# Node sums of a graph layer: from a per-window matmul to strips written to DRAM at register-held rows and read back

## The chip, the cores and the metric

One Trainium2 chip, of which the kernel uses one core with its engines: TensorE (PE, with its weight loads PEld), VectorE (DVE), ScalarE (ACT), GpSimd (POOL) and SyncE (SP). The metric is device time in microseconds (us) of one execution; a kernel's time is the median of several.

## The reference, cut to what matters

A graph layer with 6250 nodes of 256 features and 206250 edges, 33 for each node on average. The edges come sorted by their destination node. `x` first goes through a layer norm and a relu; that is the `x` of the inner function, and the original `x` is added to the result at the end.

```python
polarity = clip(edge_attr[:, 0:1], 0, 1); raw = edge_attr[:, 1:]
e = relu(raw @ W_e1.T + b_e1) @ W_e2.T + b_e2
edge_emb = (e * (polarity + 0.01)) @ W_le.T + b_le
msg = relu(x[src] + edge_emb)
aggr = segment_sum(msg, dst, num_segments=6250)
h = (x + aggr) @ W_g1.T + b_g1
out = relu(layernorm(h) * ln_g + ln_b) @ W_g2.T + b_g2
```

## The kernel before

**Tiling.** A unit `u` is 256 edges, a block is two units (512 edges), and six blocks make a group of 3072 edges; there are NU = 806 units, 403 blocks and NG = 68 groups (the last one has a single block). A group's edges are cut into S = 4 strips of 768 consecutive edges. Because the edges are sorted, the destinations of one strip lie within W = 32 consecutive nodes, from the destination of its first edge on (`base_b` holds these first nodes, as floats). A window `w` is 128 nodes; there are 49. `groups_of(w)` lists the two or three groups whose edges may end in window `w`.

**Per unit.** `edge_part` (L274, L279) multiplies the hidden features by the product of two weight matrices on TensorE, and DVE moves the result out of PSUM with a bias added (`msg`). `first_layer` (L250, with L256 on DVE and L259 on ACT) makes the hidden features two blocks at a time. `gather` (L566) fetches 128 rows of the normalised nodes by an indirect DMA that GpSimd issues; a unit takes two gathers, 1604 in all, into 20 buffers `hg`. `whole` (L615, L620) scales `msg` by the polarity and adds the gathered rows on DVE, two instructions to a unit, and ACT does the relu.

**Sums.** `rows_of_block` (L595) makes a 0/1 matrix `sel` that puts each edge of a strip at one of its 32 rows. `add_up` (L632) multiplies it with the messages, so that a group's sums gather in PSUM as 128 rows: strip `j` in rows 32j to 32j+31. `keep` copies them to `ms` (L644).

**Nodes.** For each window, `node_work` spreads the groups' rows over the window's nodes: `spread` loads `x` (L206), its transposed columns (L691) and the layer norm's two numbers for each node (L693), and makes a 128x128 0/1 matrix for each group on DVE (L698). `ready` (L707) builds the transposed node features `hT` on DVE in four instructions. `rows_of` (L732) multiplies each group's `ms` by its 0/1 matrix on TensorE, for both halves of the features, and DVE adds that to `hT` (L734). Then `first` (L170), a layer norm on DVE and ACT, `second` (two TensorE transposes, L186), `third` (L196) and the output DMA (L201, on SP).

**Order.** The program's order is written out by hand: each engine executes its instructions in the order in which the loop `for u in range(LEAD, NU)` records them, and waits by semaphores. In that loop, `forward(u)` records a unit's TensorE work; every eighth unit it also records the sums of the blocks that are complete and the next first layers and loads (`turn_of`). `whole(made)` runs `lag` units behind, and `lag` falls from 18 to 1 as `u` grows, by one for each SHRINK = 44 units. Node steps stand in `todo` by the unit at which they are due, and `due` records at most one of them per unit; small DVE steps stand in `steps` and `rest`, of which `piece` records one per unit. Gathers are recorded by `in_step`, which adds up estimated TensorE time and records a gather for each STEP = 1.288 us of it, with a wait for the TensorE instruction just recorded; where that has not yet recorded a gather that `whole` needs, `gathers(made + 1)` records it without such a wait. SP's queue, in order, carries all the loads and stores named above.

**The end.** The two last windows need the last groups. They are finished after the loop, through the lists `ending`. A check on the data (`verdict`, `count`, `total`) leads to a second, slower path if the strips do not fit.

Of the kernel before, what the change touches and what calls it, by code (L numbers as in the profile page):

```python
# [9 lines left out]
F32 = mybir.dt.float32  # L10
I32 = mybir.dt.int32
AF = mybir.ActivationFunctionType
# [5 lines left out]
P = 128  # L18
# [16 lines left out]
NT = NB * S  # L35
NG = NF + 1
NP = -(-NB // 2)
MARGIN = 768
DEG = E // N
LEAD = 22  # L40
# [9 lines left out]
TURN = 1  # L50
CH = 4
AHEAD = 10
assert DEG * N == E and NF * GE + S * P >= E


# [15 lines left out]
def groups_of(w):  # L71
    return [g for g in range(NG) if w in windows_of(g)]
# [25 lines left out]
def gnn_kernel(ctx: ExitStack, tc: tile.TileContext, x, src_c, dst_c, dst_r, pol_c, raw_t, w_e1t, w_e2,  # L98
# [50 lines left out]
    def finish_nodes(nd, ps, w, n):  # L149

        r = w * P

        def turn(a):
# [3 lines left out]
            aT = nd.tile([P, 2, P], F32, name="aT")  # L157
# [24 lines left out]

        def second(hs):
            pt = ps()
            for c in range(2):
                nc.tensor.transpose(pt[:, 0, c * P:c * P + n], hs[:n, c * P:(c + 1) * P], ident[:n, :n])  # L186
            nT = nd.tile([P, 2, P], F32, name="nT")
            for c in range(2):
                nc.scalar.activation(nT[:, c, :n], pt[:, 0, c * P:c * P + n], AF.Relu, bias=lnb_s[:, c:c + 1],  # L189
                                     scale=lng_s[:, c:c + 1])  # L190
            return nT

        def third(nT, xt):
            po = ps()
            for c in range(2):
                nc.tensor.matmul(po[:n, 0, :], nT[:, c, :n], wg2_s[:, c, :], start=c == 0, stop=c == 1)  # L196
            ot = nd.tile([P, D], F32, name="ot")
            nc.vector.tensor_add(ot[:n], po[:n, 0, :], xt[:n])
            for i, (a, b) in enumerate(spread_out(n)):
                eng = nc.scalar if i else nc.sync  # L200
                eng.dma_start(out=out[bass.ds(r + a, b - a), :], in_=ot[a:b])  # L201
# [16 lines left out]
    with fast:  # L218
# [297 lines left out]
        ends = w0.tile([P, 3], F32, name="ends")  # L516
        bad = w0.tile([P, 3], F32, name="bad")
        bad3 = w0.tile([3, 1], F32, name="bad3")

        def by_group(i, op):  # L520
            def step():
# [5 lines left out]
        def by_row(i, op):  # L527
            def step():
                nc.vector.tensor_reduce(ends[:, i:i + 1], rel, axis=AX.X, op=op)
            return step  # L530

        def verdict():
            nc.vector.scalar_tensor_tensor(far[:, 0, :], far[:, 0, :], float(DEG), mid, op0=ALU.mult, op1=ALU.subtract)
            nc.vector.scalar_tensor_tensor(far[:, 1, :], far[:, 1, :], -float(DEG), mid, op0=ALU.mult, op1=ALU.add)
            nc.vector.tensor_reduce(ends[:, 2:3], far.rearrange("p a b -> p (a b)"), axis=AX.X, op=ALU.max)
            nc.vector.tensor_scalar(bad[:, 0:1], ends[:, 0:1], float(W - 1), None, op0=ALU.is_gt)
            nc.vector.tensor_scalar(bad[:, 1:2], ends[:, 1:2], 0.0, None, op0=ALU.is_lt)
            nc.vector.tensor_scalar(bad[:, 2:3], ends[:, 2:3], float(GE // 2 + MARGIN), None, op0=ALU.is_gt)

        def count():  # L540
            pq = ps()
            nc.tensor.matmul(pq[:3, 0, 0:1], bad, ones[:, 0:1], start=True, stop=True)
            nc.vector.tensor_copy(bad3, pq[:3, 0, 0:1])

        def total():
            pq = ps()
            nc.tensor.matmul(pq[:1, 0, 0:1], bad3, ones[0:3, 0:1], start=True, stop=True)
            nc.vector.tensor_copy(bad_i, pq[:1, 0, 0:1])


        with tc.tile_pool(name="hg", bufs=HG - RAW) as hg_p, tc.tile_pool(name="ms", bufs=5) as ms_p, \
                tc.tile_pool(name="sel2", bufs=9) as sel2_p, tc.tile_pool(name="nd", bufs=3) as nd:
            got = 2 * RAW
            acc = {}
            made = 0
# [118 lines left out]
            rest = deque()  # L674
            ending = {-2: [], -1: []}

            def at(u, fn):
                todo.setdefault(max(u, now), deque()).append(fn)

            def node_work(w, spread_now=False):  # L680
# [6 lines left out]

                def spread():
                    box["xt"] = load_x()
                    box["hT"] = nd.tile([P, 2, P], F32, name="hT")  # L690
                    nc.sync.dma_start(out=box["hT"][:, :, :n], in_=x_t[:, :, w * P:w * P + n])  # L691
                    st = nd.tile([P, 2, P], F32, name="stb")
                    nc.sync.dma_start(out=st, in_=st_d[w:w + 1].to_broadcast([P, 2, P]))  # L693
                    box["st"] = st
                    box["sel2"] = []
# [82 lines left out]
            for i, fn in ((0, first_rows), (1, strips), (5, row_numbers), (6, stats_out),  # L778
                          (8, node_weights)):
                at(LEAD + i, fn)  # L780
            for i, fn in enumerate((by_group(0, ALU.max), by_group(1, ALU.min), by_row(0, ALU.max), by_row(1, ALU.min),
                                    verdict, count, total)):
                at(LEAD + 22 + 5 * i, fn)
            flag = None
            for u in range(LEAD, NU):
# [13 lines left out]
                due()  # L799
                if len(rest) > 6:  # L800
                    piece()
                if u == NU - 24:
# [1 line left out]
                        if groups_of(w)[-1] == NG - 1:  # L804
                            late[w] = node_work(w, True)
                if u == LEAD + 60:
                    flag = nc.values_load(bad_i[0:1, 0:1], min_val=0, max_val=3 * P)
            while todo:
                now = min(todo)
                for fn in todo.pop(now):  # L810
                    fn()
            while steps:
                steps.popleft()[1]()
            before, last = ending[-2], ending[-1]
# [192 lines left out]
```

## Time and profile before

| | us |
|---|---|
| median of 3 runs (lowest to highest) | 2162.19 (2161.35 to 2164.05) |
| the profiled execution's own time | 2161.02 |
| its span, first to last instruction | 2159.3 |

| engine | busy us | share of the span |
|---|---|---|
| PE | 2144.8 | 99% |
| PEld | 1613.3 | 75% |
| DVE | 1665.9 | 77% |
| ACT | 980.5 | 45% |
| POOL | 1621.5 | 75% |

The profile is one execution. A row of a group reads: line, engine, operation, output and inputs by the program's names, partitions and elements, number of instructions; then the busy time in us and the mean of one in ns; then the engine's idle time just before these instructions and what ended it. TensorE takes a 32-bit matmul in two passes, and the trace records each pass, so that a matmul counts twice (a transpose counts once). TensorE's matmuls overlap in the pipeline; the chain of waits shows how much time a run of them takes end to end. GpSimd's span for a DMA is the time in which it writes the descriptors, not the transfer. The granted TensorE clock of the execution was 0.998 of full speed.

### The profile page before, as it was taken

How to read it: one execution, taken by the hardware profiler on the slowest of the kernel's cores; microseconds unless marked ns; L12 is line 12 of the kernel's file. 1: busy time of each engine (PE TensorE's matmuls, PEld its weight loads, DVE VectorE, ACT ScalarE, POOL GpSimd, SP SyncE). 2: the span in 40 equal slices, each digit the busy share in tenths (PEclk: the TensorE clock that was granted, in tenths of full speed). 3: DMA queues.
4: the chain of work that ended last, by engine and by line, in shares of the span. 5: the costliest groups of instructions: out<-in, count | busy, mean ns of one | idle time of the engine just before them, and what ended most of it. 6: DMA issues, size and time to landing. Idle time of an engine off the chain costs nothing.

```text
span 2159.3 us, 35666 instructions
## 1 busy us (share of the span) xinstructions
PE 2144.8 (99%) x12382; PEld 1613.3 (75%) x12382; DVE 1665.9 (77%) x3975; ACT 980.5 (45%) x1710; POOL 1621.5 (75%) x1675
## 2 busy tenths in 40 slices
PE   9999999999999999999999999999999999999998
PEld 6677777777777777777777777777777777777776
DVE  7898777877777777777777777778777778777786
ACT  7544444444444444444444444444444444444443
POOL 6777777777777777777777777777777777777773
PEclk9999999999999999999999999999999999999999
DMA  9544454544445454545454445444544554454442
GB/s 312 175 134 127 141 157 135 150 137 131 140 131 148 144 149 125 152 131 149 124 151 142 133 130 153 143 133 141 147 138 125 150 151 140 128 152 131 140 138 73
DMA packets 156227, 309.23 MB, mean 143 GB/s; under 512 B 33328, under 2 KB 78089, under 8 KB 156041
## 3 DMA queue, kind: packets, MB, share of 16 engines
q0 software_dynamic: 77376, 211.39, 34.6%
q1 hardware_dynamic: 77364, 92.23, 13.6%
q10 hardware_dynamic: 1300, 3.28, 0.5%
q8 instruction: 98, 1.61, 0.3%
q14 instruction: 89, 0.72, 0.1%
HBM read 293.92 MB, written 12.85 MB: 142 GB/s over the span
## 4 chain that ended last, share of the span: by engine, by line
PE 96%; DVE 2%; DMA 1%; ACT 0%; issue 0%; SPq 0%; DVEq 0%; ACTq 0%
PE pz L274 64%; PE pz L250 17%; PE pd L632 9%; PE pz L732 3%; PE pz L170 2%; PE pz L196 2%; DMA raw<-in_raw_t_dram 1%; PE pz L186 1%; DVE hg L615 0%; DVE msg L279 0%; DVE st L141 0%; DMA xt<-in_x_dram 0%; DVE sel L595 0%; DVE mvx L142 0%; DVE msg L613 0%
## 5 line engine op out<-in xcount | busy, mean ns | idle before, releaser
L566 POOL DMA_INDIRECT hg<-hb_d,src_s x1604 | 1576.6, 983 | 493.9 <-issue 319.8
L274 PE MATMUL pz<-wc_s,e 128*128 128x256 f32 x6448 | 1452.6, 381 | 0.0
L274 PEld LDWEIGHTS pz<-wc_s,e 128*128 128x128 f32 x6448 | 1209.5, 190 | 235.2 <-ACT e L259 71.3
L620 ACT ACTIVATE hg<-hg 128x512 f32<-128x512 f32 x805 | 507.6, 631 | 862.7 <-DVE hg L615 860.9
L615 DVE SCALAR_TENSOR_TENSOR hg<-msg,pol_s,hg 128x256 f32<-128x256 f32 x1612 | 696.8, 477 | 15.6 <-DMA hg<-hb_d,src_s 14.9
L279 DVE TENSOR_TENSOR msg<-pz,bc_s 128x512 f32<-128x512 f32 x799 | 545.5, 683 | 74.0 <-PE pz L274 73.7
L256 DVE TENSOR_SCALAR e<-pz,vecs 128x512 f32<-128x512 f32 x201 | 150.8, 750 | 361.1 <-PE pz L250 361.0
L259 ACT ACTIVATE e<-pz,vecs 128x512 f32<-128x512 f32 x605 | 361.1, 691 | 148.4 <-PE pz L250 148.3
L250 PE MATMUL pz<-raw,we_s 64*128 64x512 f32 x1612 | 379.3, 604 | 3.7 <-DVE msg L279 2.0
L250 PEld LDWEIGHTS pz<-raw,we_s 64*128 64x128 f32 x1612 | 148.5, 187 | 188.2 <-issue 155.4
L632 PE MATMUL pd<-hg,sel 128*32 128x256 f32 x3216 | 194.9, 382 | 0.6 <-ACT hg L620 0.6
L632 PEld LDWEIGHTS pd<-hg,sel 128*32 128x32 f32 x3216 | 94.4, 109 | 87.8 <-issue 34.9
L595 DVE SCALAR_TENSOR_TENSOR sel<-iota_w,zero_c,rel 128x128 f32<-128x128 f32 x403 | 137.3, 341 | 0.0
L644 ACT ACTIVATE ms<-pd 128x256 f32<-128x256 f32 x66 | 25.2, 382 | 127.2 <-PE pd L632 127.1
L732 PEld LDWEIGHTS pz<-s,ms 128*128 128x128 f32 x548 | 68.7, 192 | 3.1 <-PE pd L632 0.4
L732 PE MATMUL pz<-s,ms 128*128 128x128 f32 x548 | 69.3, 275 | 0.1
L707 DVE SCALAR_TENSOR_TENSOR hT<-hT,zero_c,stb 128x128 f32<-128x128 f32 (+1 forms) x196 | 66.7, 341 | 3.0 <-DMA stb<-st_d 3.0
L196 PE MATMUL pz<-wg_s,nT 128*128 128x256 f32 (+1 forms) x196 | 50.6, 380 | 0.6 <-ACT nT L189 0.6
L170 PE MATMUL pz<-wg_s,hT 128*128 128x256 f32 (+1 forms) x196 | 50.5, 380 | 0.0
L392 POOL TENSOR_TENSOR hb<-xt,rows_b 128x256 f32<-128x256 f32 (+1 forms) x49 | 34.1, 728 | 10.5 <-ACT xt L388 3.0
L196 PEld LDWEIGHTS pz<-wg_s,nT 128*128 128x128 f32 (+1 forms) x196 | 37.0, 190 | 6.2 <-ACT nT L189 0.8
L170 PEld LDWEIGHTS pz<-wg_s,hT 128*128 128x128 f32 (+1 forms) x196 | 37.0, 190 | 5.7 <-issue 0.3
(98 smaller groups left out, 412.8 us busy)
## 6 DMA issues: line engine op xcount, KB each, us to landing
raw<-in_raw_t_dram SPq DMA_DIRECT2D x202, 256.0 KB
hg<-hb_d,src_s POOLq DMA_INDIRECT x1604
stb<-st_d SPq DMA_DIRECT2D x49, 128.0 KB
hb_d<-hb SPq DMA_DIRECT2D x12, 512.0 KB
xt<-in_x_dram SPq DMA_DIRECT2D x48, 128.0 KB
hT<-in_x_t_dram SPq DMA_DIRECT2D x48, 128.0 KB
out_dram<-ot SPq DMA_DIRECT2D x48, 128.0 KB
xt<-in_x_dram SPq DMA_DIRECT2D x11, 512.0 KB
```

The source lines that it names most:

```text
L196: nc.tensor.matmul(po[:n, 0, :], nT[:, c, :n], wg2_s[:, c, :], start=c == 0, stop=c == 1)
L250: z = nc.tensor.matmul(pe[s, c], we1_s[s * F:(s + 1) * F, c * P:(c + 1) * P], raw[q][s * F:(s + 1) * F, :], start=True, stop=True)
L256: nc.vector.tensor_scalar(e1[b][:, c, :], pe[s, c], be1_s[:, c:c + 1], 0.0, op0=ALU.add, op1=ALU.max)
L259: nc.scalar.activation(e1[b][:, c, :], pe[s, c], AF.Relu, bias=be1_s[:, c:c + 1])
L274: last_z = nc.tensor.matmul(pz[:, i, :], e1[b][:, c, k:k + P], wc_s[:, c, :], start=c == 0, stop=c == 1)
L279: nc.vector.tensor_add(msg[u], pz, bc_s)
L566: g = nc.gpsimd.indirect_dma_start(out=hg[u][:, i, :], out_offset=None, in_=hb_d, in_offset=bass.IndirectOffsetOnAxis(ap=src_s[:, 2 * u + ...
L595: nc.vector.scalar_tensor_tensor(sel[g][:, k * S:(k + 1) * S, :], iota_w.rearrange("p (o w) -> p o w", o=1).to_broadcast([P, S, W]), zero_ ...
L615: nc.vector.scalar_tensor_tensor(hg[u][:, i, :], m[:, i, :], pol_s[:, 2 * u + i:2 * u + i + 1], hg[u][:, i, :], op0=ALU.mult, op1=ALU.add)
L620: nc.scalar.activation(hg[u], hg[u], AF.Relu)
L632: z = nc.tensor.matmul(acc[g][j * W:(j + 1) * W, :], sel[g][:, k * S + j, :], m[:, j % 2, :], start=k == 0, stop=b == blocks_of(g)[-1])
L732: nc.tensor.matmul(pa[:, c, :n], ms[g][:, c * P:(c + 1) * P], box["sel2"][i][:, :n], start=i == 0, stop=i == len(gs) - 1)
```

## The change

Of the windows, the 47 whose groups all lie before group FAR = 66 are done in another way (`far_work`); the last two are done as before.

- Two arrays in DRAM, `sum_d[0]` and `sum_d[1]`, hold one row of 256 numbers for each node. `clear` writes zeros to a window's rows in both, some groups ahead of its first group.
- When a group's `ms` is there, `rows_out` reads the four strips' first nodes from `base_i` (an integer copy of `base_b`) into SP's registers and writes each strip's 32 rows with a DMA on SP, at the row that the register holds: strips 0 and 2 to the one array, 1 and 3 to the other. Two strips that follow each other may share a node; those of one array may not, and a fourth term in the check on the data covers that.
- `far_work` makes the layer norm's and relu's output for the window's nodes again from `x` on ACT, reads the window's rows of both arrays with two DMAs, adds them with two DVE instructions, transposes the sum with two TensorE transposes (`turn`, copied out of PSUM by ACT), and goes on with `first`, `second` and `third`.
- The matmuls `rows_of`, the 0/1 matrices, the transposed load of `x`, the load of the layer norm's numbers and the steps `ready` fall away for these windows.
- The node steps counted by `due` go from five to four for each window. `piece` now takes the first step that is due, not only the head of the queue. Pools `ms` and `sel2` have fewer buffers (4 and 6 for 5 and 9), and `hT` and `stb` come from a pool of two.

```diff
+FAR = NG - 2
+CLEAR = 4
+    sum_d = [dram.tile([N + W, D], F32, name=f"sum_d{i}") for i in range(2)]
...
+            nc.vector.tensor_copy(base_i, base_b[0:1].rearrange("p g j -> p (g j)"))
+            nc.vector.memset(zrow, 0.0)
...
+        def strips_apart():
+            flat = base_b.rearrange("p g j -> p (g j)")
+            n = FAR * S - 2
+            nc.vector.tensor_tensor(apart[:, :n], flat[:, 2:n + 2], flat[:, :n], ALU.subtract)
+            nc.vector.tensor_reduce(ends[:, 3:4], apart[:, :n], axis=AX.X, op=ALU.min)
...
             def piece():
-                if steps and steps[0][0] <= now:
-                    steps.popleft()[1]()
+                due_now = [s for s in steps if s[0] <= now][:1]
+                if due_now:
+                    steps.remove(due_now[0])
+                    due_now[0][1]()
                 elif rest:
                     rest.popleft()[1]()
...
                     sel.pop(g)
+                    if g < FAR:
+                        soon(1, lambda: rows_out(g, 0))
+                        soon(2, lambda: rows_out(g, 1))
                     for w in range(NW):
-                        if groups_of(w)[-1] == g:
+                        if groups_of(w)[0] == g + CLEAR:
+                            soon(6, lambda w=w: clear(w))
+                        if groups_of(w)[-1] == g < FAR:
+                            far_work(w)
+                        elif groups_of(w)[-1] == g:
                             late.pop(w)()
-                        elif groups_of(w)[-1] == g + 1 < NG - 1:
+                        elif groups_of(w)[-1] == g + 1 == FAR:
                             late[w] = node_work(w)
...
+            def soon(n, fn):
+                moves.setdefault(now + n, []).append(fn)
+            def clear(w):
+                if groups_of(w)[-1] < FAR:
+                    for i in range(2):
+                        nc.sync.dma_start(out=sum_d[i][w * P:(w + 1) * P, :], in_=zrow)
+            def rows_out(g, k):
+                if k == 0:
+                    _, firsts[g] = nc.values_load_multi_w_load_instructions(
+                        base_i[0:1, g * S:(g + 1) * S], engines=[mybir.EngineType.SP], min_val=0, max_val=N)
+                for i in range(2):
+                    j = 2 * k + i
+                    nc.sync.dma_start(out=sum_d[i][bass.ds(firsts[g][j], W), :], in_=ms[g][j * W:(j + 1) * W, :])
+            def far_work(w):
+                box = {}
+                turn, first, second, third, load_x, offset = finish_nodes(nd, ps, w, P)
+                def h_of_x():
+                    box["xt"] = load_x()
+                    box["h"] = nh.tile([P, 2, P], F32, name="stb").rearrange("p a b -> p (a b)")
+                def load():
+                    nc.scalar.activation(box["h"], box["xt"], AF.Relu, bias=nm_s[:, w:w + 1], scale=rs_s[:, w:w + 1])
+                    box["ab"] = ab_p.tile([P, 2, D], F32, name="ab")
+                    for i in range(2):
+                        nc.sync.dma_start(out=box["ab"][:, i, :], in_=sum_d[i][w * P:(w + 1) * P, :])
+                def add(i):
+                    nc.vector.tensor_add(box["h"], box["h"], box["ab"][:, i, :])
+                def turned():
+                    box["hT"] = turn(box["h"], nh, "hT")
+                    at(now + 2, one)
+                def one():
+                    box["hs"] = first(box["hT"])
+                    at(now + 5, two)
+                def two():
+                    box["nT"] = second(box["hs"])
+                    at(now + 4, lambda: third(box["nT"], box["xt"]))
+                soon(1, h_of_x)
+                soon(4, load)
+                steps.extend((now + 6, lambda i=i: add(i)) for i in range(2))
+                steps.extend((now + 7, lambda c=c: offset(box["xt"], c)) for c in range(2))
+                at(now + 9, turned)
```

More of the change, by code (lines that the diff above doesn't have):

```diff
@@ L151, in finish_nodes, with turn @@
         r = w * P
-        def turn(a):
+        def turn(a, pool=nd, name="aT"):
             pt = ps()
@@ L156, in turn @@
                 nc.tensor.transpose(pt[:, 0, c * P:c * P + n], a[:n, c * P:(c + 1) * P], ident[:n, :n])
[L157 removed]
+            aT = pool.tile([P, 2, P], F32, name=name)
             if n == P:
@@ L512, in row_numbers @@
                 nc.vector.tensor_scalar(rowid[q], base_b[q, :, j], p32[q], None, op0=ALU.add)
+            nc.vector.tensor_copy(base_i, base_b[0:1].rearrange("p g j -> p (g j)"))
+            nc.vector.memset(zrow, 0.0)
         far = w0.tile([P, 2, NG], F32, name="far")
-        ends = w0.tile([P, 3], F32, name="ends")
-        bad = w0.tile([P, 3], F32, name="bad")
-        bad3 = w0.tile([3, 1], F32, name="bad3")
+        ends = w0.tile([P, 4], F32, name="ends")
+        bad = w0.tile([P, 4], F32, name="bad")
+        bad4 = w0.tile([4, 1], F32, name="bad4")
+        apart = w0.tile([P, FAR * S], F32, name="apart")
         def by_group(i, op):
@@ L538, in verdict @@
             nc.vector.tensor_scalar(bad[:, 2:3], ends[:, 2:3], float(GE // 2 + MARGIN), None, op0=ALU.is_gt)
+            nc.vector.tensor_scalar(bad[:, 3:4], ends[:, 3:4], float(W), None, op0=ALU.is_lt)
         def count():
             pq = ps()
-            nc.tensor.matmul(pq[:3, 0, 0:1], bad, ones[:, 0:1], start=True, stop=True)
-            nc.vector.tensor_copy(bad3, pq[:3, 0, 0:1])
+            nc.tensor.matmul(pq[:4, 0, 0:1], bad, ones[:, 0:1], start=True, stop=True)
+            nc.vector.tensor_copy(bad4, pq[:4, 0, 0:1])
         def total():
             pq = ps()
-            nc.tensor.matmul(pq[:1, 0, 0:1], bad3, ones[0:3, 0:1], start=True, stop=True)
+            nc.tensor.matmul(pq[:1, 0, 0:1], bad4, ones[0:4, 0:1], start=True, stop=True)
             nc.vector.tensor_copy(bad_i, pq[:1, 0, 0:1])
-        with tc.tile_pool(name="hg", bufs=HG - RAW) as hg_p, tc.tile_pool(name="ms", bufs=5) as ms_p, \
-                tc.tile_pool(name="sel2", bufs=9) as sel2_p, tc.tile_pool(name="nd", bufs=3) as nd:
+        with tc.tile_pool(name="hg", bufs=HG - RAW) as hg_p, tc.tile_pool(name="ms", bufs=4) as ms_p, \
+                tc.tile_pool(name="sel2", bufs=6) as sel2_p, tc.tile_pool(name="ab", bufs=2) as ab_p, \
+                tc.tile_pool(name="nh", bufs=2) as nh, tc.tile_pool(name="nd", bufs=3) as nd, \
+                tc.tile_pool(name="nk", bufs=1) as nk:
+            base_i = nk.tile([1, NG * S], I32, name="base_i")
+            zrow = nk.tile([P, D], F32, name="zrow")
             got = 2 * RAW
@@ L689, in spread @@
                     box["xt"] = load_x()
-                    box["hT"] = nd.tile([P, 2, P], F32, name="hT")
+                    box["hT"] = nh.tile([P, 2, P], F32, name="hT")
                     nc.sync.dma_start(out=box["hT"][:, :, :n], in_=x_t[:, :, w * P:w * P + n])
-                    st = nd.tile([P, 2, P], F32, name="stb")
+                    st = nh.tile([P, 2, P], F32, name="stb")
                     nc.sync.dma_start(out=st, in_=st_d[w:w + 1].to_broadcast([P, 2, P]))
@@ L780, in gnn_kernel @@
                 at(LEAD + i, fn)
+            now = LEAD
+            for w in range(NW):
+                if groups_of(w)[0] < CLEAR:
+                    soon(8, lambda w=w: clear(w))
             for i, fn in enumerate((by_group(0, ALU.max), by_group(1, ALU.min), by_row(0, ALU.max), by_row(1, ALU.min),
-                                    verdict, count, total)):
+                                    strips_apart, verdict, count, total)):
                 at(LEAD + 22 + 5 * i, fn)
@@ L799, in gnn_kernel @@
                 due()
+                for fn in moves.pop(now, []):
+                    fn()
                 if len(rest) > 6:
@@ L806, in gnn_kernel @@
                 if u == LEAD + 60:
-                    flag = nc.values_load(bad_i[0:1, 0:1], min_val=0, max_val=3 * P)
+                    flag = nc.values_load(bad_i[0:1, 0:1], min_val=0, max_val=4 * P)
             while todo:
@@ L811, in gnn_kernel @@
                     fn()
+            assert not moves
             while steps:
```

2 lines of the change are left out of this document (added).

## The prediction

> **What bounds the kernel now.** The page came first: the span and the engines' busy time.
>
> ```profile
> span 2159.3 us, 35666 instructions
> PE 2144.8 (99%) x12382; PEld 1613.3 (75%) x12382; DVE 1665.9 (77%) x3975; ACT 980.5 (45%) x1710; POOL 1621.5 (75%) x1675
> ```
>
> TensorE looks like the only bound, and GpSimd a quarter idle. The groups and the waits of the gathers correct that:
>
> ```profile
> L566 POOL DMA_INDIRECT hg<-hb_d,src_s x1604 | 1576.6, 983 | 493.9 <-issue 319.8
> L566 POOL DMA_INDIRECT hg<-hb_d,src_s x1604: 942/946/1963, 65.3 to 2131.8; - x179
> 2131.85 0.95 POOL L566 DMA_INDIRECT hg<-hb_d,src_s  x1 [0.30 <-issue]
> ```
>
> The 1604 gathers start at 65.3 and the last ends at 2132.8: 2067.5 us, or 1.289 us each. Of that 0.983 is the instruction and 493.9 / 1604 = 0.308 the pause before it. The pause is 0.30 before nearly every one and counts as issue. So GpSimd runs from end to end as well: its idle quarter is the pause between gathers, and no wait can be taken out of it. Two engines are full together.
>
> The chain of waits in the middle of the span, on TensorE alone, is the other bound; two turns of eight units each:
>
> ```profile
> 901.89 1.86 PE pd L632 x32
> ...
> 911.04 1.34 PE pz L732 x12
> ...
> 925.47 3.63 PE pz L250 x16
> 929.10 3.65 PE pz L274 x16
> 932.75 0.22 PE pz L186 x2
> ...
> 944.20 1.86 PE pd L632 x32
> ```
>
> From 901.89 to 944.20, 42.31 us pass for 16 units, 21.16 to a turn, without a gap. How fast do gathers feed a turn? `lag` falls by one in 44 units, so a turn takes 16 x 45/44 = 16.36 gathers: 21.09 us at 1.289. The two rates differ by 0.07 us in 21.
>
> **What the gathers cost, in stretches.** I cut the span at starts of gathers and counted those within:
>
> ```profile
> 140.25:371.61 231.36, 176.23 (x181) 1.00 0.48 137
> 371.61:800.55 428.94, 327.47 (x333) 1.00 0.49 141
> 800.55:1200.17 399.62, 305.17 (x310) 1.00 0.48 139
> 2000.79:2133.00 132.21, 100.45 (x102) 1.00 0.46 136
> ```
>
> Length over count: 1.278, then 1.288 and 1.289. The waits of DVE for a gather's data stand in the first stretch:
>
> ```profile
> DVE hg L615 <- DMA hg<-hb_d,src_s: 13.3, 20, 1.8
> DVE hg L615 <- DMA hg<-hb_d,src_s: 1.6, 2, 1.2
> L615 DVE SCALAR_TENSOR_TENSOR hg<-msg,pol_s,hg x1612: 466/477/552, 71.7 to 2143.9; 128x256 f32<-128x256 f32 x180
> ```
>
> The first line is the window 140 to 371, the second 371 to 2130. So data came just in time early on, and later GpSimd drew ahead; by the third line, which has the first and last start of L615, the last one stands 11 us behind the last gather.
>
> Why does a gather last 0.95 at one time and 1.2 at another? The timeline of the two engines:
>
> ```profile
> 1033.87 0.95 POOL L566 DMA_INDIRECT hg<-hb_d,src_s  x1 [0.30 <-ACT e L259]
> 1034.22 1.67 DVE L615 SCALAR_TENSOR_TENSOR hg<-msg,pol_s,hg 128x256 f32<-128x256 f32 x4
> 1035.12 1.19 POOL L566 DMA_INDIRECT hg<-hb_d,src_s  x1 [0.30 <-issue]
> 1042.79 0.87 DVE L615 SCALAR_TENSOR_TENSOR hg<-msg,pol_s,hg 128x256 f32<-128x256 f32 x2
> 1042.87 1.22 POOL L566 DMA_INDIRECT hg<-hb_d,src_s  x1 [0.30 <-issue]
> ```
>
> Where an L615, whose inputs all lie in SBUF, runs over a gather's start, the gather is 0.24 to 0.27 longer; where it starts well after (1034.22, 0.35 into the gather before), it is not. Summed: 1576.6 - 1604 x 0.946 = 59 us of lengthening, 0.037 for each of 1612 L615.
>
> The Trainium skill has a rule for this, in SBUF — State Buffer, SBUF: two separate sides: a DVE instruction with two SBUF inputs can hold the port pair that DVE and GpSimd share against a GpSimd operation that reads SBUF, and the loser blocks for the whole instruction. The trace agrees, at 0.24 to 0.27 us a hit. It speaks against this change, whose added sums on DVE have two such inputs; by the whole of a 0.42 us instruction for each of 94, the sum would lose 39 us, where the price from rows below is 3.5.
>
> **The change, part by part.**
>
> *TensorE.* The 47 windows hold 134 window-group pairs; two halves and two passes make 536 of the 548 records of
>
> ```profile
> L732 PE MATMUL pz<-s,ms 128*128 128x128 f32 x548 | 69.3, 275 | 0.1
> ```
>
> At 1.34 / 12 = 0.112 (chain above) that is 59.9 us removed. Two transposes for each window come in, 94 at 0.22 / 2 = 0.11: 10.3. Net 49.5 us, all of it on TensorE's path; a turn loses (1.34 - 0.22) / 2 = 0.56 and takes 20.6. If TensorE alone set the end, the span would be 2159.3 - 49.5 = 2109.8.
>
> *GpSimd.* Nothing is taken from it: 1604 gathers, the same start. A turn now needs 20.6 on TensorE and 20.91 (at 1.278) to 21.09 on GpSimd. TensorE gains 0.3 to 0.5 us a turn on the gathers. In the first stretch the lead over DVE's use is a few us at most, so it is gone after some ten turns, near 350 to 450 us, and from there GpSimd alone sets the pace. The added NODES estimates fall from five to four per window, so `in_step` records gathers too slowly and `gathers(made + 1)` records them without a wait; GpSimd, always behind, loses nothing by it.
>
> *Pace of the gathers.* What is new is the lead: small to the end, as in the stretch 140 to 371. When DVE waits for data, L615 starts at a fixed point:
>
> ```profile
> 155.69 0.95 POOL L566 DMA_INDIRECT hg<-hb_d,src_s  x1 [0.30 <-issue]
> 158.19 0.95 POOL L566 DMA_INDIRECT hg<-hb_d,src_s  x1 [0.30 <-issue]
> 158.48 0.48 DVE L615 SCALAR_TENSOR_TENSOR hg<-msg,pol_s,hg 128x256 f32<-128x256 f32 x1 [0.22 <-DMA hg<-hb_d,src_s]
> ```
>
> 1.84 us after its gather's end, 0.29 into a later gather, past the point where it would lengthen it. Bounds for the remaining 1368 gathers (after 371.6): none lengthened, 0.946 + 0.302 = 1.248, and as now, 1.288. I take 1.278, the stretch that the new state is nearest to: 1368 x (1.288 - 1.278) = 13 us gained. The last gather then ends at 2120.
>
> *The end.* The sums of units 800 to 803 start here:
>
> ```profile
> 2138.31 0.87 DVE L615 SCALAR_TENSOR_TENSOR hg<-msg,pol_s,hg 128x256 f32<-128x256 f32 x2
> 2139.06 1.93 PE L632 MATMUL pd<-hg,sel 128*32 128x256 f32 x32
> ```
>
> 6.3 us after the last gather. They need unit 803, whose second gather is four before the last: 5.1 earlier, plus 1.84 to arrive, 0.48 (L615) and 0.63 (L620), 2.1 us before the last gather's end. Between nothing (the lead stays) and 8.4 us fall away; I take 6.5, 8.4 less the longest wait for data above (1.8).
>
> *DVE and ACT.* Removed: 134 of L698, 188 of L707, 47 of L734; added: 94 sums, 47 relus of `x` and 47 copies on ACT:
>
> ```profile
> L698 DVE TENSOR_SCALAR s<-iota_p,rowid 128x128 f32<-128x128 f32 x140 | 31.6, 289 | 0.0
> L707 DVE SCALAR_TENSOR_TENSOR hT<-hT,zero_c,stb 128x128 f32<-128x128 f32 (+1 forms) x196 | 66.7, 341 | 3.0 <-DMA stb<-st_d 3.0
> L734 DVE SCALAR_TENSOR_TENSOR hT<-hT,pz 128x256 f32<-128x256 f32 x48 | 19.6, 409 | 0.0
> L388 ACT ACTIVATE xt<-xt,nm_s,rs_s 128x256 f32<-128x256 f32 (+1 forms) x49 | 25.4, 590 | 7.1 <-DVE nm_s L385 6.9
> ```
>
> DVE loses 38.7 + 64.1 + 19.2 = 122 and gains 94 x 0.41 (L734, of the same width) = 39; ACT gains at most 94 x 0.59 = 55. Both stay under 80% busy and behind the gathers: nothing, unless a gather has to wait for them. Of lengthening, the sums bring 94 x 0.037 = 3.5; the 188 L707, also with SBUF inputs alone, take between nothing and 7 with them: I take nothing for both.
>
> *SP and the arrays.* For each group of some 32 us: a register load, four strip writes; for each window two zero writes and two reads for two loads dropped.
>
> ```profile
> L807 SPq TENSOR_LOAD <-bad_i x1: 485/485/485, 216.8 to 216.8; - x1
> L693 SPq DMA_DIRECT2D stb<-st_d x49: 361/598/981, 98.9 to 2109.8; - x49
> SPq L201 <- DVE ot L198: 1383.9, 48, 36.6
> ```
>
> At 0.5 and 0.6 each that is about 5 us of issue to a group, in a queue that idles 1384 us behind L201 alone. Strip 2 must wait until strip 0 has landed, and the reads for both; queued behind them stand `raw` loads a turn (21 us) ahead of their use. Three transfers in a row, at 1.84 (as for the gather above) to 3.6 (with the longest wait added), end 6 to 11 us after `ms`; the sums stand six units later, behind six runs of L274 at 3.65 / 2 and the first layers' 3.63, some 14 us. So DVE finds them there: nothing. Without that cover DVE would stand still before each, and behind it `msg`, PSUM and TensorE; the longest such wait in the whole run, 2.3 us, is for `stb`:
>
> ```profile
> DVE hT L707 <- DMA stb<-st_d: 3.0, 3, 2.3
> ```
>
> That 47 times is 108 us, the upper bound.
>
> **Sum.** 2159.3 - 13 - 6.5 = 2139.8. The profiled execution took 2161.02, 1.7 more than its span, and the median is 1.2 above that: 2143.
>
> **The rivals.**
>
> *GpSimd's pace stays.* The lengthening stays at 1.288, since later stretches with very different leads all show it: 2152.8 + 2.9 = 2156. Against it, the stretch with waits.
>
> *TensorE's gain arrives.* If waiting DVE locks itself to the free point, gathers come near 1.248 and TensorE, at 2109.8, becomes the bound: 2113, or up to 2128 on the way. Against it: sums and first layers give DVE bursts of work that start at any point.
>
> *Slower: DVE locks to the wrong point.* With GpSimd alone in front, every further hit on a gather's start is paid in full. If L615 and the new sums hit twice as often, 1368 x 0.040 = 55 us come on top of what now lies there: 2159 + 55 - 6.5 + 2.9 = 2210. It turns the sign once the mean of the gathers passes 1.288 + 6.5 / 1368 = 1.293. For it: 2000 to 2133 shows 1.296. Against it: the locked point seen at 158.48 is free.
>
> *Late arrays.* The sums wait for the reads and TensorE stands behind DVE for all of it: 2109.8 + 108 + 2.9 = 2221. It decides from (2139.8 - 2109.8) / 47 = 0.64 us a window on, and is slower than before from 1.05 on. Against it, the 14 us against 11. That the second path runs instead would cost a multiple; two strips on, the first nodes are 2 x 768 / 33 = 46 apart against 32 allowed, so I leave it out.
>
> **How the numbers follow.** Forecast 0.52, pace stays 0.18, TensorE's gain 0.16, wrong point 0.10, late arrays 0.04. 0.2% is 4.3 us, about what this measurement tells from no change: faster lies under 2157.9. All of forecast and TensorE's gain and two in five of "pace stays" are faster: 0.75; the rest of that is the same, 0.11; slower 0.14. The range 2118 to 2166 leaves out the lower part of TensorE's gain and the slower cases, some 0.2; the forecast's own is 2130 to 2152.
>
> **What would show it.** Right: gathers still without a pause beyond 0.30, some 1.278 apart after 371 us; TensorE with about 30 us of gaps, at L632 above all; DVE's waits for gathers in the hundreds of times; L732 with 12 records; the last L615 within 5 us of the last gather. Wrong: pauses before gathers, TensorE without gaps, DVE waiting for `ab` or TensorE for `raw`.

## The result, and the profile after

| | before | after |
|---|---|---|
| median, us (lowest to highest, 4 runs each, side by side) | 2161.95 (2161.35 to 2164.05) | 2239.06 (2237.6 to 2241.49) |
| after over before, 95% interval | | 1.0356 [1.0338, 1.0374] |
| the profiled execution, us | 2161.02 | 2237.6 |
| its span | 2159.3 | 2235.5 |

The change makes the kernel 3.6% slower; 2143 was predicted. In the changed program a gather stands at L584, the scaling of the messages (L615 before) at L635, the first layers at L253 (L250), their relu on ACT at L262 (L259), `edge_part` at L277 (L274), `add_up` at L652 (L632), the added sums at L741. The page after, its first lines and the groups of the gathers and the sums:

```profile
span 2235.5 us, 35993 instructions
PE 2155.1 (96%) x11940; PEld 1583.1 (71%) x11940; DVE 1631.6 (73%) x3705; ACT 1008.7 (45%) x1804; POOL 1603.5 (72%) x1675
L584 POOL DMA_INDIRECT hg<-hb_d,src_s x1604 | 1558.7, 972 | 599.6 <-issue 368.7
L741 DVE TENSOR_TENSOR stb<-stb,ab 128x256 f32<-128x256 f32 x94 | 39.4, 419 | 1.0 <-DMA ab<-sum_d 1.0
```

TensorE, 99% busy before, now stands still for 80 us (2235.5 - 2155.1). The gathers themselves became shorter, 972 ns against 983, but the idle time before them grew from 493.9 to 599.6. The answer for line 584 has the first and the last start:

```profile
L584 POOL DMA_INDIRECT hg<-hb_d,src_s x1604: 940/946/2069, 63.7 to 2218.4; - x179
```

The last one ends at 2218.4 + 0.94 = 2219.3. With these rows and those of before the whole difference can be laid out along GpSimd:

| | before | after | difference |
|---|---|---|---|
| start of the first gather | 65.3 | 63.7 | -1.6 |
| the gathers' own time | 1576.6 | 1558.7 | -17.9 |
| pauses before them | 493.9 | 599.6 | +105.7 |
| from the last gather's end to the span's end | 26.5 | 16.2 | -10.3 |
| sum | | | +75.9 |

The spans differ by 76.2. (Each column adds up to some 3 us more than its span, since the pause before the first gather lies ahead of its start.) So everything that is lost stands in pauses before gathers, and it hides a gain of 30 in the other rows. GpSimd's waits after, by what ended them:

```profile
POOL hg L584 <- issue: 368.7, 1126, 4.7
POOL hg L584 <- PE pz L253: 58.9, 80, 8.9
POOL hg L584 <- ACT e L262: 52.0, 64, 8.7
```

Pauses of up to 8.9 us, ended by first layers on TensorE or by ACT behind them; before, nearly every pause was 0.30. The windows of line 584 show where they are (length, busy time and count of the gathers, granted clock, DMA share, GB/s):

```profile
321.00:580.00 259.00, 197.42 (x202) 1.00 0.53 154
800.00:1200.00 400.00, 257.99 (x269) 0.96 0.45 132
1200.00:1450.00 250.00, 165.27 (x173) 0.94 0.45 134
1450.00:1800.00 350.00, 266.39 (x275) 1.00 0.52 152
1800.00:2218.00 418.00, 318.17 (x328) 1.00 0.50 148
```

A gather every 1.28 us up to 580, every 1.49 from 800 to 1200 and 1.45 to 1450, and every 1.27 from there to the end. What is lost is lost in the middle and then stops. One such pause in the timeline:

```profile
1159.90 0.94 POOL L584 DMA_INDIRECT hg<-hb_d,src_s  x1 [0.30 <-issue]
1164.49 1.93 PE L652 MATMUL pd<-hg,sel 128*32 128x256 f32 x32
1166.36 3.70 PE L253 MATMUL pz<-raw,we_s 64*128 64x512 f32 x16
1169.12 0.94 POOL L584 DMA_INDIRECT hg<-hb_d,src_s  x1 [8.28 <-ACT e L262]
1171.94 0.48 DVE L635 SCALAR_TENSOR_TENSOR hg<-msg,pol_s,hg 128x256 f32<-128x256 f32 x1 [0.80 <-DMA hg<-hb_d,src_s]
```

GpSimd does nothing for 8.28 us. In the program this gather is recorded by `in_step` behind unit 417's first layers, so it carries a wait for them; it begins near the end of their run (1166.36 to 1170.06). (The trace puts the release down to their relu on ACT, L262, for which the program gives it no wait.) And the rows it fetches are the next that DVE needs: L635 starts 1.88 after its end, and had itself waited 0.80 for them. The wait that keeps gathers in step with TensorE here holds back a gather that is already late.

TensorE's windows around it, after:

```profile
63.70:580.00 516.30, 510.93 (x2892) 1.00 0.51 152
580.00:1450.00 870.00, 808.75 (x4341) 0.96 0.45 134
1450.00:2218.00 768.00, 763.85 (x4385) 1.00 0.51 150
```

61 of TensorE's 80 idle us lie in the stretch with the pauses. Of the 80, 42.6 stand before `first` (L173), which waits there for ACT's copy of `hT` (L162). In the same stretch the granted clock is 0.96, against 1.00 on both sides. The Trainium skill, TensorE: Matmul & The Clock Gate, in its part on the HAM clock gate, says that the array falls to half clock after a window of some 3.4 us without work; the trace agrees so far that the lower clock stands only where TensorE idles. How much of the 76 us the clock adds is not separated by any run here; and since the gaps and the lower clock stand together, these rows do not show which brought the other.

### The profile page after: what moved, and what is told of

Same layout as the page of the kernel before. It is cut to its first block, busy times and chain, and to the rows that moved or that the text cites. A ratio compares the mean times of both kernels' runs of the same rounds, so it can differ in the third digit from the quotient of the medians.

```text
span 2235.5 us, 35993 instructions
## 1 busy us (share of the span) xinstructions
PE 2155.1 (96%) x11940; PEld 1583.1 (71%) x11940; DVE 1631.6 (73%) x3705; ACT 1008.7 (45%) x1804; POOL 1603.5 (72%) x1675
## 5 line engine op out<-in xcount | busy, mean ns | idle before, releaser
L584 POOL DMA_INDIRECT hg<-hb_d,src_s x1604 | 1558.7, 972 | 599.6 <-issue 368.7
L277 PE MATMUL pz<-wc_s,e 128*128 128x256 f32 x6448 | 1467.1, 384 | 0.0
L277 PEld LDWEIGHTS pz<-wc_s,e 128*128 128x128 f32 x6448 | 1220.9, 192 | 241.8 <-ACT e L262 74.6
L635 DVE SCALAR_TENSOR_TENSOR hg<-msg,pol_s,hg 128x256 f32<-128x256 f32 x1612 | 729.1, 480 | 337.2 <-DMA hg<-hb_d,src_s 333.0
L253 PE MATMUL pz<-raw,we_s 64*128 64x512 f32 x1612 | 407.2, 614 | 19.7 <-DVE msg L282 18.8
L262 ACT ACTIVATE e<-pz,vecs 128x512 f32<-128x512 f32 x605 | 360.7, 693 | 66.1 <-PE pz L253 65.9
L253 PEld LDWEIGHTS pz<-raw,we_s 64*128 64x128 f32 x1612 | 157.3, 187 | 221.4 <-issue 118.8
L259 DVE TENSOR_SCALAR e<-pz,vecs 128x512 f32<-128x512 f32 x201 | 150.6, 749 | 212.3 <-PE pz L253 211.9
L652 PE MATMUL pd<-hg,sel 128*32 128x256 f32 x3216 | 199.5, 382 | 2.8 <-ACT hg L640 2.5
L652 PEld LDWEIGHTS pd<-hg,sel 128*32 128x32 f32 x3216 | 95.5, 109 | 93.5 <-issue 35.3
L173 PE MATMUL pz<-wg_s,hT 128*128 128x256 f32 (+1 forms) x196 | 58.8, 427 | 42.6 <-ACT hT L162 42.6
L173 PEld LDWEIGHTS pz<-wg_s,hT 128*128 128x128 f32 (+1 forms) x196 | 37.4, 206 | 57.2 <-ACT hT L162 50.9
L741 DVE TENSOR_TENSOR stb<-stb,ab 128x256 f32<-128x256 f32 x94 | 39.4, 419 | 1.0 <-DMA ab<-sum_d 1.0
L192 ACT ACTIVATE nT<-pz,vecs 128x128 f32<-128x128 f32 (+1 forms) x98 | 38.6, 444 | 2.5 <-PE pz L189 2.5
L214 DVE SCALAR_TENSOR_TENSOR xt<-xt,zero_c,rows_b 128x128 f32<-128x128 f32 (+1 forms) x98 | 33.5, 343 | 0.0
```

What stands on the lines that cost most here:

```text
L253: z = nc.tensor.matmul(pe[s, c], we1_s[s * F:(s + 1) * F, c * P:(c + 1) * P], raw[q][s * F:(s + 1) * F, :], start=True, stop=True)
L259: nc.vector.tensor_scalar(e1[b][:, c, :], pe[s, c], be1_s[:, c:c + 1], 0.0, op0=ALU.add, op1=ALU.max)
L262: nc.scalar.activation(e1[b][:, c, :], pe[s, c], AF.Relu, bias=be1_s[:, c:c + 1])
L277: last_z = nc.tensor.matmul(pz[:, i, :], e1[b][:, c, k:k + P], wc_s[:, c, :], start=c == 0, stop=c == 1)
L584: g = nc.gpsimd.indirect_dma_start(out=hg[u][:, i, :], out_offset=None, in_=hb_d, in_offset=bass.IndirectOffsetOnAxis(ap=src_s[:, 2 * u + ...
L635: nc.vector.scalar_tensor_tensor(hg[u][:, i, :], m[:, i, :], pol_s[:, 2 * u + i:2 * u + i + 1], hg[u][:, i, :], op0=ALU.mult, op1=ALU.add)
```

## The experiments

In two of the four sets of runs every kernel, the one before too, took 18 to 48% longer than the same kernel in the other two, so each ratio is against the kernel before in the same set. Sets two and four, where the kernel before takes 2162 and 2163 us as in the result, come first; the other two follow.

**Theory.** `due` adds NODES to `spent` for every node step, and `in_step` records gathers by `spent`. With four steps for a window in place of five, `spent` falls behind by 0.65 us with each window. A gather is named here by the unit whose rows it fetches. At 16.4 units a window, some 15.1 windows have passed by unit 248, where the first pause over 1 us after the start stands (at 697.7 us): 9.8 us, or 7.6 gathers at 1.288. From there `in_step` reaches a gather only in the very unit in which `whole` needs it, and still gives it the wait. Once `spent` is further behind, `gathers(made + 1)` comes first, without a wait, and the pauses end. Going through the loop in the program's order with these amounts, 175 gathers are recorded by `in_step` with a wait in the very unit that needs them, 166 of them for units 203 to 464; in the program before it is one, and with 0.8125 (f1) none. Matched in this order with the 1604 gathers of the trace, the pauses beyond 0.30 us add up to 106.6 us before these 175, to 3.5 before the 341 others that have the wait, and to 3.1 before the 919 that are as late but have none. So it takes both, the lateness and the wait. **Rivals:** DVE or the reads of the sums are late; or the sums and moved instructions hit GpSimd.

**f1: the estimate restored.** Nothing else is changed.

```diff
-EDGE, LAYER, SUMS, NODES = 1.754, 0.9, 0.46, 0.65
+EDGE, LAYER, SUMS, NODES = 1.754, 0.9, 0.46, 0.8125
```

> The changed kernel with NODES 0.8125 instead of 0.65 once more, for a chip on which the kernel before runs at 2160 us as in the result. There theory A (gathers recorded at the unit that needs them, with a wait for TensorE, hold GpSimd up) gives 2125 to 2143: no pause beyond 0.30 us before gathers, 1.27 to 1.28 us from one to the next. Theory B (buffers) and theory C (the arrays' transfers) give over 2180. On a chip on which the kernel before takes some 2556 us, as in the first set, engines wait for issue and the change of the estimate gives the time of before within 1%.

2140.73 us (2139.66 to 2142.61) against 2162.09: 0.9901 [0.9884, 0.9917]. The page of f1, its first lines, the gathers' group, and the answers for line 584 and for its windows:

```profile
span 2139.7 us, 36355 instructions
PE 2113.9 (99%) x11940; PEld 1569.2 (73%) x11940; DVE 1623.0 (76%) x3705; ACT 1009.7 (47%) x1804; POOL 1612.5 (75%) x1675
L584 POOL DMA_INDIRECT hg<-hb_d,src_s x1604 | 1567.6, 977 | 493.3 <-issue 322.3
L584 POOL DMA_INDIRECT hg<-hb_d,src_s x1604: 942/946/2066, 65.4 to 2122.4; - x179
800.00:1200.00 400.00, 304.64 (x314) 1.00 0.52 151
```

The pauses are back at 493.3, the 400 us with 269 gathers now hold 314, and the clock is 1.00 there. One constant takes away all of the loss, and the change that remains is worth 1%. TensorE has the same matmuls in both programs, and 41 us more of busy time in the one (2155.1 against 2113.9), whose mean granted clock is lower (0.984 against 0.996). The wait of L173 for L162 falls from 42.6 to 8.1 us.

**f2: no gather waits for TensorE**, with NODES at 0.65 as in the change.

```diff
-                    gather(behind)
-                    behind = None
+                    gather()
```

> The changed kernel without the gathers' wait for TensorE once more. By the part of the changed kernel's trace after unit 470, where no gather has that wait and they stand 1.273 us apart, 2125 to 2145. By the first set of runs, where it was 1.24 times the kernel before, over 2500: then gathers that run ahead hurt on every chip, and the part after unit 470 was spared only because GpSimd stood just ahead of their use.

2141.08 us (2137.11 to 2142.06), 0.9896 [0.988, 0.9913]. Here the estimate is as low as in the change and only the waits are gone; the time is f1's. So it is the wait on late gathers that costs, not their place in the order.

**f3: the kernel before with a low estimate**, five steps at 0.52, the same 0.65 short for each window; nothing of the change is in it.

```diff
-EDGE, LAYER, SUMS, NODES = 1.754, 0.9, 0.46, 0.65
+EDGE, LAYER, SUMS, NODES = 1.754, 0.9, 0.46, 0.52
```

> The kernel before with NODES 0.52 once more. Theory A: pauses before gathers between units 200 and 420 and none later, 2210 to 2270 where the kernel before takes 2160. Theories B and C: no change.

2239.06 us (2236.68 to 2242.26), 1.0355 [1.0338, 1.0373]: the time of the changed kernel, out of the kernel before. Its gathers:

```profile
L566 POOL DMA_INDIRECT hg<-hb_d,src_s x1604 | 1567.6, 977 | 586.2 <-issue 360.1
800.00:1310.00 510.00, 337.89 (x350) 0.97 0.43 125
1310.00:2218.00 908.00, 691.28 (x704) 1.00 0.48 139
```

The same picture, with 172 late gathers by the program's order: one gather per 1.46 us from 800 to 1310, then 1.29. Matched with the trace, 81.8 us of pauses beyond 0.30 us stand before these 172 and 15.2 before others that have the wait. After the start, the pauses over 2 us stand at units 239 to 423, as expected; five of 1.1 to 1.4 us come sooner, from unit 112 on. Strips, arrays, sums and DVE's changed work are not needed for the loss. That the median is the changed kernel's to the digit is chance: this kernel loses 77 us against its own right estimate, the changed one 98.

**h2: an estimate between the two**, NODES at 0.72. `spent` then falls behind by 5 x 0.65 - 4 x 0.72 = 0.37 us a window.

> The changed kernel with NODES 0.72: estimates of a window between those of 0.65 (2239 us) and 0.8125 (2141). In program order some 320 gathers are recorded at the unit that needs them and still wait for TensorE, later than with 0.65 (units 250 to 790 instead of 60 to 460). Theory of the late, waiting gathers, at 95 to 109 us lost in some 175 of them, 0.55 to 0.62 each: 2290 to 2340 us, slower than 0.65, with pauses of several us between units 250 and 790. Rival, time goes smoothly with the estimate: 2180 to 2200. Rival, NODES acts only by a few marginal places: within 1% of 2141.

2247.45 us (2241.77 to 2252.68), 1.0379 [1.0353, 1.0404]: closer to the right estimate, and no faster. The gathers' windows of h2:

```profile
800.00:1200.00 400.00, 302.79 (x311) 1.00 0.51 151
1200.00:1600.00 400.00, 292.27 (x302) 1.00 0.50 146
1600.00:2000.00 400.00, 247.92 (x261) 0.94 0.43 126
L584 POOL DMA_INDIRECT hg<-hb_d,src_s x1604 | 1559.4, 972 | 609.8 <-issue 383.6
```

The pauses come later. The first over 1 us after the start stands at unit 438 (1185.9 us): 26.7 windows at 0.37 are 9.9 us short, as the changed kernel's 15.1 at 0.65 were 9.8. In these two the place follows the arrears, as the theory says, while f3's small pauses came at less; both rivals in the expectation are out. The size that I gave does not hold: 324 gathers late in the program's order instead of 175 cost 117 us of pauses (609.8 - 493.3) instead of 106, so each late one costs 0.36 instead of 0.61, and the time was below the 2290 expected. The loss is no fixed price for each. Matched with the trace, the difference lies with the gathers that wait for first layers: beyond 0.30 us they pause for 1.45 us on average in the changed kernel (50 of them) and for 0.44 in h2 (64), where those behind `edge_part` pause for 0.28 (99) and 0.36 (201).

**h1: less work on TensorE**, f1 with half of `third` left out; the output lacks the second half of the last product's sum.

```diff
-                nc.tensor.matmul(po[:n, 0, :], nT[:, c, :n], wg2_s[:, c, :], start=c == 0, stop=c == 1)
+                if c == 0:
+                    nc.tensor.matmul(po[:n, 0, :], nT[:, c, :n], wg2_s[:, c, :], start=True, stop=True)
```

> The changed kernel with NODES 0.8125, and the second of the two matmuls of `third` left out (the output lacks half of the last product): 0.4 us less TensorE work to a strip's third layer, some 50 to 100 us in all. On a chip on which the kernel before takes some 2160 us, with gathers 0.30 us apart. If the gathers alone set the end (they ran from 65.4 to 2123.3 us, 1.281 us each, in f1): no change, 2138 to 2143 us, and TensorE shows the time as gaps. If TensorE is still the bound beside them: below 2125.

2140.51 us (2136.4 to 2142.53), 0.9887 [0.987, 0.9903]. The first lines of its page and the gathers' group:

```profile
span 2140.8 us, 36159 instructions
PE 2100.6 (98%) x11842; PEld 1546.7 (72%) x11842; DVE 1626.3 (76%) x3705; ACT 1008.1 (47%) x1804; POOL 1614.6 (75%) x1675
L585 POOL DMA_INDIRECT hg<-hb_d,src_s x1604 | 1569.7, 979 | 493.1 <-issue 332.3
```

TensorE does 13.3 us less (less than the 50 to 100 that I expected to take away) and idles 40.2 instead of 25.8; the time stays. With the estimate right, the gathers alone set the end.

**h3: each zero write twice**, in f1: 94 more DMAs on SP.

> The changed kernel with NODES 0.8125 and each zero write issued twice, so 94 more DMAs on SP. If SP's queue and the arrays are hidden behind other work, as the sums' waits for `ab` (1.0 us in all) say: 2139 to 2144 us. If they lie on the path: at least 0.5 us for each of 94, 2188 or more.

2145.84 us (2144.35 to 2151.44), 0.9915 [0.9899, 0.9932]: 5.1 us over f1, a little above the range for hidden writes and far below 2188. But the kernel before is 1.3 us longer in this set as well, and f1's interval against it (0.9884 to 0.9917) overlaps this one, so no cost of the writes is clear of the noise. The gathers of its page, which is that of the longest of the four executions:

```profile
L584 POOL DMA_INDIRECT hg<-hb_d,src_s x1604 | 1574.4, 982 | 493.8 <-issue 322.9
```

They are longer by 6.8 us in all (1574.4 against 1567.6) with the pauses unchanged, and the sums' wait for `ab` is 1.1 (0.4 in f1). So the added writes delay nothing that waits for them; whether the longer gathers come from the writes was not tried.

**h4: the kernel before without the wait at paced gathers**, the edit of f2.

> The kernel before without the wait for TensorE at paced gathers. If the kernel before loses nothing to that wait where gathers are 0.30 us apart (no pauses beyond 0.30 in its trace): 2155 to 2165. If the 1% that f1 gains came from the pace and not from TensorE's removed work: 2135 to 2145.

2162.34 us (2161.22 to 2165.34), 0.9997 [0.9987, 1.0006]. The kernel before loses nothing to its pace here, so the 1% of f1 and f2 belongs to the change.

**The two sets with longer times.** In the first, the kernel before took 2556.39 us (2546.93 to 2576.63). It held the kernels of f1, f2, f3 and h4:

> The changed kernel with NODES 0.8125 instead of 0.65, so that four node steps add up to what five did (3.25 us a window); nothing else. Theory A (the pace: gathers recorded at the very unit that needs them, with a wait for TensorE, hold GpSimd up): the pauses of 108.7 us before gathers are gone, gathers 1.27 to 1.28 us apart throughout, the last gather ends near 2110 to 2120, the time is 2125 to 2143. Theory B (gathers wait for one of the 20 buffers, which TensorE's sums free late): pauses stay, 2220 to 2245. Theory C (the arrays' transfers delay the gathers' data): pauses may go but DVE's waits for gathers stay above 300 us with late data, over 2180.

> The changed kernel with in_step recording its gathers without the wait for TensorE. Theory A: as with the larger estimate, no pause beyond 0.30 us, 2125 to 2145. Theory B: the buffers bind as before, 2220 to 2245. Theory C: over 2180.

> The kernel before with NODES 0.52, so that five node steps add up to the 2.6 us that the changed kernel's four do; no DRAM arrays, all of the old matmuls. Theory A: pauses before gathers in units 200 to 420, some 60 to 110 us, and a time of 2210 to 2270. Theories B and C: no change, 2158 to 2166.

> The kernel before with in_step recording its gathers without the wait for TensorE. Theory A: its gathers run back to back already, so 2150 to 2165, and what this gives up against the changed kernel without the wait is the change's own gain. Rival: the wait is there for a reason of its own (gathers that run ahead hit more of DVE's work), and the time rises above 2166.

e1 2567.73 us, 1.0027 [0.9994, 1.006]; e2 3161.34, 1.2382 [1.2326, 1.2438]; e3 2871.68, 1.1229 [1.1172, 1.1285]; e4 3084.07, 1.2046 [1.1991, 1.2102]. The low estimate costs the kernel before 12% here, but e1 is level with the kernel before, so that of the change's own 1% nothing shows; and the kernels without the wait, expected to be the fast ones, were the slowest. With the kernel before at 2556, the ranges given in us decide nothing. The third set, with before at 2593.84 (2581.67 to 2601.07), held the kernels of h1, h4, h3 and h2:

> The changed kernel with NODES 0.8125, and the second of the two matmuls in third left out (the output lacks half of the last product): 49 matmuls of 0.43 us, 21 us less on TensorE. If GpSimd alone sets the pace, the time stays within 5 us of 2141; if TensorE still counts, it falls to some 2120 to 2130.

> The kernel before without the gathers' wait for TensorE, for a chip on which the kernel before takes 2160 us: its gathers run back to back already, so 2150 to 2165. Then the gain of the changed kernel with the larger estimate, 1%, belongs to the change and not to the pace. If it falls to 2145 or below, the gain was the pace's.

> The changed kernel with NODES 0.8125 and every write of zeros done twice: 94 more DMAs of 128 KB on SP. If the arrays' traffic is hidden, the time stays within 5 us of 2141; if it is paid (later data for gathers, a fuller queue on SP), it rises by 10 us or more.

> The changed kernel with NODES 0.72, between 0.65 and 0.8125. By the order in which the program records them, 324 gathers then have a wait for TensorE and no unit of lead, in units 250 to 790 (175 in units 60 to 460 of the changed kernel with 0.65; none with 0.8125). Theory A: no pauses before unit 250, pauses from some 350 to 790, and a time above the changed kernel's 2239, 2240 to 2330, although the estimate is nearer to the good one. If only the size of the estimate counted, it would lie between, near 2190.

g1 2602.17 us, 1.0031 [1.001, 1.0052]; g2 3176.51, 1.2226 [1.2154, 1.2298]; g3 2606.56, 1.0043 [1.0016, 1.0071]; g4 2644.74, 1.019 [1.0151, 1.0229]. For what bounds the kernel in the result these two sets are inconclusive, and the other two decide. What they show by themselves is told at the end.

## Why the prediction was wrong

**The step that failed** stands under *GpSimd*: "The added NODES estimates fall from five to four per window, so `in_step` records gathers too slowly and `gathers(made + 1)` records them without a wait; GpSimd, always behind, loses nothing by it." The edit was seen and its first half is right: `spent` falls behind by 0.65 a window. The second half holds too, but only later. On the way there is a stretch, with its pauses over 1 us at units 248 to 464, in which `in_step` still comes first, with gathers that are already needed, and gives them the wait. That was costed at nothing; it measured 106.3 us of pauses (599.6 against f1's 493.3). The step went from the first state (ahead, with waits) to the last (behind, without) and left out the one between. No rival held it; "pauses before gathers" was named as the sign that the prediction is wrong, and it is the row that showed it.

**The rest of the sum held**, as f1 shows, which is the change with that one step made true. The predicted span was 2139.8 and f1's is 2139.7:

| term | predicted | f1 against before |
|---|---|---|
| gathers, less lengthening | -13 | 1567.6 - 1576.6 = -9.0 |
| from the last gather to the end | -6.5 | 16.3 - 26.5 = -10.2 |

The two errors cancel: the pace gained 4 us less, the end 3.7 more. That the spans agree to 0.1 us is luck.

- *What bounds the kernel*: right. h1 shows that less work on TensorE changes nothing once the gathers alone are in front. The sign that was named for it came out only in part: f1's TensorE idles 25.8 us, but 14.5 of that stood there before (2159.3 - 2144.8), and most of its waiting is not at the sums but at L173, 8.1 us in 14 waits.
- *Pace of the gathers*: right in kind. f1's 1604 gathers from 65.4 to 2123.4 come every 1.283 us, between the 1.278 taken and the 1.288 of before. In f1's trace 409 gathers begin while a scaling runs and lose 42.6 us by it, for 464 and 53.3 before, so the lengthening fell as argued. DVE's waits for gathers are in the hundreds, and f1's last scaling starts 3 us behind the last gather; the waits of f1 and of after:

```profile
DVE hg L635 <- DMA hg<-hb_d,src_s: 250.2, 314, 2.9
DVE hg L635 <- DMA hg<-hb_d,src_s: 333.0, 406, 3.4
```

- *TensorE*: of the per-window matmuls 24 records are left on two lines (one row below), and 94 transposes are there at the price taken: f1's chain of waits has 0.22 us for two, at 922.18. (The 18.0 us of the row below are busy time, in which the transposes that were there before also have 18.8 for 98.) Yet TensorE's busy time fell by 30.9 us (2144.8 to 2113.9) and not by 49.5; the first layers alone are 9.2 longer (388.5 against 379.3). That does not reach the end, since TensorE does not set it.

```profile
L816 PE MATMUL pz<-s,ms 128*128 128x128 f32 x12 | 1.5, 275 | 0.0
L159 PE MATMUL pz<-ident,stb 128*128 128x128 f32 x94 | 18.0, 273 | 1.2 <-DVE stb L741 1.2
```

- *SP and the arrays*, and the rival *late arrays*: the sums wait 1.0 us in the whole run (L741 above), not 108. Right, with h3 beside it.
- The rival *DVE locks to the wrong point* is out: gathers became shorter, 972 and 977 ns against 983, though the 94 sums were added. The sums' own price can be read from f1's trace: 36 gathers begin while one of them runs, and these are 3.0 us longer in all than at 0.946 each. That is near the 3.5 from the rows and far from the 39 us that the prediction worked out by the rule of the Trainium skill (SBUF — State Buffer, SBUF: two separate sides), the whole instruction for each of the 94; here the measurement decides. *GpSimd's pace stays* and *TensorE's gain arrives* are out as well, by f1's 2140.7 against 2156 and 2113 to 2128.

Not settled: what share of the loss the lower clock carries, and why a late gather behind first layers costs 1.45 us in the one kernel and 0.44 in the other.

## What to carry to other kernels

Where a program's order is steered by sums of estimated times, an edit that drops or adds steps changes the sum for all that follows: give the new steps the old total, and it is an edit of one constant (here worth 98 us, more than four times the gain of the change). When an order drifts from one regime to another, go through the loop for the places between, and ask of each instruction that it records whether it still carries a wait that made sense only while it was early. The version with NODES at 0.8125 beats both kernels, at 0.9901 of the one before, where that one takes 2162 us.

## What the runs showed of the hardware

In the first and third set the same program took 2556 and 2594 us where it took 2162 and 2163 in the others; the first and the fourth set ran on the same chip, so it is not a fixed trait of a chip. The kernels without the pace, level with the others at 2141 and 2162 us, lost another 20 to 24% there. The granted clock was lower as well: 0.871 in e4's profiled execution, 0.997 in h4's. Rows of e4's page, its waits among them, beside h4's, the same kernel:

```profile
L274 PE MATMUL pz<-wc_s,e 128*128 128x256 f32 x6448 | 1760.3, 419 | 442.3 <-issue 423.7
POOL hg L566 <- issue: 881.5, 1329, 16.3
DVE msg L279 <- remote: 519.8, 104, 12.9
```

```profile
L274 PE MATMUL pz<-wc_s,e 128*128 128x256 f32 x6448 | 1454.4, 381 | 0.0
POOL hg L566 <- issue: 332.9, 1092, 0.3
```

("Remote" is a releaser that the profile cannot name.) GpSimd stands for up to 16.3 us, DVE for up to 12.9 and TensorE for 423.7 in all without an instruction in the trace that ends the wait. There the wait that keeps the gathers in step with TensorE is worth a fifth; in the other sets it is worth nothing. What held the engines up is not shown, and no run here tells why gathers that run ahead make it worse.
